# Attention scores from high and low halves of q and k in single-pass products, in a decoder layer whose instruction order is planned

## The chip, the cores and the metric

The kernel runs on one core of a Trainium2 chip. The metric is the device time of one execution in microseconds (us). The engines are TensorE (PE; PEld is its loading of the stationary operand), VectorE (DVE), ScalarE (ACT), GpSimd (POOL) and SyncE (SP), which here only issues the transfers.

## The reference

The layer has three parts, each followed by a residual sum and a layernorm, for 32 sequences of 256 tokens and 256 channels.

```python
x = layernorm(x + mamba(x))            # state-space block, 512 inner channels, 16 states, chunks of 64
x = layernorm(x + cross_attention(x, ctx_1024))
x = layernorm(x + experts(x))          # 8 experts by position, 256 -> 704 -> 256, silu(gate) * up

# the state-space block: u = silu(conv(x W_in)), delta = softplus(...), then for each chunk of 64
carry = exp(delta * A) * carry + delta * B * u         # over the tokens of the chunk
y = sum_n(carry * C);  y = y * silu(res);  out = y W_out

# the cross attention, 16 heads of 16 channels
scores = q k^T / sqrt(16);  attn = softmax(scores);  out = (attn v) W_o
```

All inputs and outputs are float32.

## The kernel before

**The order is planned.** The whole program is one pool of work that the author writes as generators ("chains"), one for each kind of work: `pres` and `steps` (projections and sizes of the state-space block), `decays`, `scan`, `weighted` and `sums` (the recurrence), `mixes` (output projection and first layernorm), `queries`, `keys_ahead`, `keys`, `maxima`, `attns`, `finishes` (attention), and for the experts `fetches`, `inputs`, `units` and `seconds`, twice. When the program is built, `in_order` keeps an account of the time on each engine. `spend` adds a duration to an engine, the yields tell when a chain can go on and on which engine it issues next, and the chain that can start first is stepped. The order of the instructions on every engine is what comes out, and it is fixed. The durations of the account are constants (`MM`, `EV`, `VE`, `CV`, `GP`, and numbers in the calls of `spend`). All transfers go through SyncE's one queue, in the order of the account (`dma`).

**The recurrence** has 512 steps, 16 for each sequence. A step loads delta and delta*u spread over 128 partitions (`ld`, two transfers of 256 KB), ScalarE takes the exponents (`da`, L573), VectorE multiplies (`bu`, L602) and scans 1024 elements (`h`, L621), GpSimd multiplies `h` by C (L637), and after four steps TensorE sums the states (`y`, L651) and VectorE gates the sum (`yg`, L667). Loads run three steps ahead, six `h` buffers exist.

**Attention.** Each sequence's q and k are made as 256 channels x 256 tokens (`q_flat`, `k_flat`, by `biased`), written to DRAM (`heads`, `k_all`) and read back by `spread_heads` into `qT` and `kT`. These have 64 rows for each head (`HR`), two heads side by side on the partitions (rows 0 and 64) and eight groups along the free axis. Of a head's 64 rows 16 hold its channels, the rest are zero in `qT`; `kT` has a one in row 63. `maxima` makes the scores of two heads in one call of `scores` (four products of 128x256, contraction over 63 rows), VectorE takes the maximum of each query (`tops`, L838), TensorE transposes the maxima, ScalarE negates them (`rows`, L847), and they go through DRAM into row 63 of `qT`. Then `attns` calls `scores` with k on the left, over 64 rows, so that the product holds score minus maximum, and ScalarE takes the exponent (`es`, L894). The products with v (`ps_oT`, L863) give output and sum together. A half of the heads (8) is one unit of this work. `scored` tells when a half of `qT` and `kT` can be overwritten.

**Experts.** 32 units of work (UNITS) of 256 columns; the last eight handle two experts on 128 columns each. A unit needs the finished second layernorm of its sequences, of the last four for the last four units. `ps_h` (L1133) and `ps_down` (L1212) are its products. They have the lowest rank when banks of PSUM are handed out (`take`; five banks).

The change touches `heads` (weights of q and k at the start), `rest`, `spread_heads`, `keys_ahead`, `queries`, `scores`, `maxima`, `attns`, a buffer of `finish` and the constants.

Of the kernel before, what the change touches and what calls it, by code (L numbers as in the profile page):

```python
# [7 lines left out]

F32 = mybir.dt.float32
AF = mybir.ActivationFunctionType  # L10
ALU = mybir.AluOpType
AX = mybir.AxisListType
# [3 lines left out]
P = 128  # L16
B, L, D = 32, 256, 256
# [5 lines left out]
NQ = NS // NL  # L23
GB = 2
# [8 lines left out]
NG = 4  # L33
# [64 lines left out]
def decoder_kernel(ctx: ExitStack, tc: tile.TileContext, a: dict, out: bass.AP):  # L98
# [4 lines left out]
    def dma(dst, src):  # L103

        nc.sync.dma_start(dst, src)
        spend("SP", ISSUE)
# [10 lines left out]

    k_all = dram.tile([B, D, L], F32, name="k_all")
    v_all = dram.tile([B, L, D], F32, name="v_all")

# [44 lines left out]

    def heads(n):

        w = wp.tile([P, 2, D], F32, tag="w_" + n, name="w_" + n)
        src = a["w_" + n].rearrange("(k p) (h c) -> p k h c", p=P, c=32)
        for k in range(2):  # L170
            dst = w[:, k].rearrange("p (h c) -> p h c", c=DK)
            dma(dst, src[:, k, :, :DK])
        bias = wp.tile([P, 2], F32, name="b_" + n)
        for g in range(NG):
            r = 64 * (g % 2)
            src = a["b_" + n].rearrange("(j c) g -> j c g", c=32)[:, :DK, g : g + 1]
            dma(bias[r : r + 64, g // 2 : g // 2 + 1], src)
        return w, bias
# [29 lines left out]

    later = []
    now, dma = dma, lambda dst, src: later.append((dst, src))  # L210
    w_k, b_k = heads("k")
    w_v = weight("w_v", D, D)
    b_out = row("b_out")
    w_out = weight("w_out", DI, D)
    w_q, b_q = heads("q")
    w_o = weight("w_o", D, D)
# [53 lines left out]

    kT = keep.tile([P, HG, L], F32, name="kT")
    last = small.tile([P, 1], F32, tag="ln_st", name="last")
    at = ident.rearrange("p (j c) -> p j c", c=HR)[:, :, HR - 1]
    nc.vector.tensor_reduce(last, at, AX.X, ALU.add)
    nc.vector.tensor_copy(kT.rearrange("p g t -> p (g t)"), last.to_broadcast([P, HG * L]))
    qT = keep.tile([P, HG, L], F32, name="qT")
    nc.gpsimd.memset(qT, 0.0)

# [27 lines left out]

    MM = 0.47
    EV = {1: 0.47, 2: 0.6, 4: 1.06}
    VE = {1: 0.41, 2: 0.69, 4: 1.23}
    CV = 0.565  # L310
    GP = {1: 0.7, 2: 1.27, 4: 2.36}

    def layernorm(tiles, t):

        n = len(tiles)
        mv = small.tile([P, n, 2], F32, tag="ln_mv", name="ln_mv")
        for i, x in enumerate(tiles):
            st = small.tile([P, 6], F32, tag="ln_st", name="ln_st")
            nc.vector.bn_stats(st, x)
            nc.vector.bn_aggr(mv[:, i, :], st)  # L320
        yield spend("DVE", 0.6 * n, t), "POOL"
        rstd = small.tile([P, n, 1], F32, tag="ln_rstd", name="ln_rstd")
        nc.gpsimd.tensor_scalar_add(rstd, mv[:, :, 1:2], EPS)  # L323
        nc.gpsimd.tensor_tensor(rstd, rstd, power[:, :n, :], ALU.pow)
        off = small.tile([P, n, 1], F32, tag="ln_off", name="ln_off")
        nc.gpsimd.tensor_tensor(off, mv[:, :, 0:1], rstd, ALU.mult)
        nc.gpsimd.tensor_scalar_mul(off, off, -1.0)
        yield spend("POOL", 1.5), "ACT"
        for i, x in enumerate(tiles):
            nc.scalar.activation(  # L330
                x, x, AF.Identity, bias=off[:, i, :], scale=rstd[:, i, :]
            )
        return spend("ACT", 0.6 * n)

# [29 lines left out]
    def rest():  # L364

        while later:
            yield 0.0, "SP"
            dma(*later.pop(0))

    xps, dds, sress, bcds, ygs, us, spread, silus = {}, {}, {}, {}, {}, {}, {}, []  # L370
# [175 lines left out]
    def decays():  # L546
# [15 lines left out]
        for i in range(STEPS):  # L562
# [8 lines left out]
            for g in range(GB):  # L571
                for q in range(NQ):
# [5 lines left out]
                    )  # L578
            decayed[i] = spend("ACT", GB * NQ * 0.5)

    read = {-1: 0.0}

    def scan():
# [4 lines left out]
        for i in range(STEPS):  # L588
# [39 lines left out]
            )  # L628
            recurred[i] = spend("DVE", 2.29)
            read[i] = max(multiplied, decayed[i])  # L630
# [45 lines left out]
    scored = {}  # L676

    def spread_heads(b, dst, d, t, there):

        yield t, "SP"  # L680
        for half in range(2):
            if b:
                yield lambda: max(t, scored[b - 1, half]) if (b - 1, half) in scored else None, "SP"
            for j in range(2):
                src = d.rearrange("(i g j c) t -> i j c g t", i=2, j=2, c=DK)[half, j]
                dma(dst[HR * j : HR * j + DK, 4 * half : 4 * half + 4, :], src)
            there[b, half] = clock.at["SP"] + LANDING
# [3 lines left out]
    def keys_ahead():  # L691

        for b in range(B):
# [14 lines left out]
            done(1, tk)  # L708
            yield tk, "SP"
            dma(k_all[b].rearrange("(m p) t -> p m t", p=P), flat)  # L710
            yield from take(1, rank, t0)
# [77 lines left out]
    def queries():  # L789
        for b in range(B):  # L790
# [12 lines left out]
            done(1, tq)  # L803
            yield tq, "SP"
            d = bcd.tile([D, L], F32, tag="heads", name="heads")
            dma(d.rearrange("(m p) t -> p m t", p=P), flat)
            yield from spread_heads(b, qT, d, clock.at["SP"] + LANDING, qts)

    def scores(heads, left, right, n):


        ss = [bank("s").rearrange("p (t n) -> p t n", t=2) for _ in heads]
        for t in range(2):
            for h, s in zip(heads, ss):
                g, r = h // 2, HR * (h % 2)
                nc.tensor.matmul(  # L816
                    s[:, t, :],
                    left[r : r + n, g, t * P : (t + 1) * P],
                    right[r : r + n, g, :],
                    start=True,  # L820
                    stop=True,
                )
        return ss, spend("PE", 2 * MM + 0.2)

    def maxima():

        for i in range(2 * B):
# [5 lines left out]
            while h < 8:  # L833
                yield from take(2, 2, t0)
                ss, ts = scores(range(8 * half + h, 8 * half + h + 2), qT, kT, HR - 1)
                for s in ss:
# [8 lines left out]
            yield spend("PE", 0.2), "ACT"  # L845
            rows = unit2.tile([H, P], F32, tag="rows", name="rows")
            nc.scalar.activation(rows, ps, AF.Identity, scale=-1.0)  # L847
            t = spend("ACT", 0.35)
            done(1, t)
            yield t, "SP"  # L850
            d = bcd.tile([2, 4 * L], F32, tag="tops", name="tops")
            dma(d.rearrange("j (i n) -> (j i) n", n=P), rows)
            yield clock.at["SP"] + LANDING, "SP"
            dst = qT[HR - 1 :: HR, 4 * half : 4 * half + 4]
            dma(dst.rearrange("j g t -> j (g t)"), d)
            tts[b, half] = clock.at["SP"] + LANDING
# [17 lines left out]
    def attns():  # L874

        for n in range(2 * B):
# [4 lines left out]
            for g in range(3):  # L881
                ess = []
                while g < 2 and len(ess) < 4:
                    yield from take(2, 2, tq)
                    h = 8 * half + 4 * g + len(ess)
                    ss, ts = scores(range(h, h + 2), kT, qT, HR)
                    if g and not ess:
# [36 lines left out]
    def finish(b):  # L924
# [27 lines left out]
        yield t, "ACT"  # L952
        aT = unit1.tile([P, 2, L], F32, tag="aT", name=f"aT_{b}")
        nc.scalar.copy(aT, ps)
# [387 lines left out]
```

## Time and profile before

| what | value |
|---|---|
| median of 3 runs | 2744.92 us (2738.03 to 2745.47) |
| the profiled execution | 2743.78 us |
| its span, first to last instruction | 2742.0 us |
| TensorE busy | 2466.3 us, 90% |
| VectorE busy | 2380.6 us, 87% |
| ScalarE busy | 2043.4 us, 75% |
| GpSimd busy | 1643.7 us, 60% |
| moved by DMA | 505.86 MB, 64.8% of the 16 engines' time |
| mean granted clock of TensorE | 0.959 |

"Busy" for TensorE counts a product from its start to the modelled end, so overlapping products count once, and a wide busy time is not the same as full use. A line of the group and timeline views gives line, engine, operation, output<-inputs, shapes and count; a line of the waits gives who waited for whom, the microseconds in total, how often, and the longest. A float32 product is two records in the trace, each with its own load.

### The profile page before, as it was taken

To read this page: it belongs to the slowest core of one execution; us is meant where nothing else is said; L and a number is where in the kernel's file an instruction comes from. 1 tells how busy PE (TensorE), PEld (TensorE's weight loads), DVE (VectorE), ACT (ScalarE), POOL (GpSimd) and SP (SyncE) were. 2 spreads that over 40 slices of the span, in tenths; PEclk is the share of its full clock that TensorE was granted. 3 is DMA by queue.
4 is the path that set the end of the run, shared out by engine and by line. 5 is a ranking of instruction groups with operands and counts; after the bars stand their busy time and mean duration, and the time that the engine had idled before them with its cause. 6 is when DMAs were issued, how large, how long until landed. Compare 5 with 4: busy or idle time off the path is not lost.

```text
span 2742.0 us, 48659 instructions
## 1 busy us (share of the span) xinstructions
PE 2466.3 (90%) x16964; PEld 1705.3 (62%) x16964; DVE 2380.6 (87%) x2413; ACT 2043.4 (75%) x4327; POOL 1643.7 (60%) x1145
## 2 busy tenths in 40 slices
PE   5788989889899899989998989999999899998988
PEld 4565666566566666666666666665666566666767
DVE  4999999999999999999999999999999899896212
ACT  6887888888778878887878778888788788674331
POOL 4775766666666666575666665666666666553000
PEclk8899999999999999998999999999999999999999
DMA  7866666666676666676666666667666566666464
GB/s 203 228 199 176 193 187 181 189 191 191 187 199 186 181 167 190 176 197 177 167 198 187 198 175 186 187 177 195 190 197 179 163 172 180 185 174 181 150 195 144
DMA packets 491497, 505.86 MB, mean 184 GB/s; under 512 B 177204, under 2 KB 339252, under 8 KB 491252
## 3 DMA queue, kind: packets, MB, share of 16 engines
q1 hardware_dynamic: 491252, 502.75, 64.8%
q8 instruction: 135, 2.21, 0.4%
q14 instruction: 110, 0.90, 0.1%
HBM read 426.07 MB, written 76.55 MB: 183 GB/s over the span
## 4 chain that ended last, share of the span: by engine, by line
PE 29%; DVE 11%; ACT 8%; DMA 5%; issue 3%; POOL 1%; SPq 1%; DVEq 0%; ACTq 0%; POOLq 0%
PE ps_h L1133 8%; PE s L816 6%; DVE h L621 5%; PE ps_down L1212 4%; ACT da L573 3%; PE y L651 3%; DVE bu L602 2%; DVE tops L838 2%; PE ps_in L349 2%; PE ps_oT L863 2%; DMA ld<-dd 1%; DMA xe<-x2d 1%; PE ps_out L349 1%; PE ps_qk L349 1%; ACT es L894 1%
## 5 line engine op out<-in xcount | busy, mean ns | idle before, releaser
L637 POOL TENSOR_TENSOR h<-h,c_bc 128x1024 f32<-128x1024 f32 x512 | 1209.1, 2362 | 740.6 <-DVE h L621 627.0
L621 DVE TENSOR_TENSOR_SCAN h<-da,bu 128x1024 f32<-128x1024 f32 x512 | 1168.9, 2283 | 50.4 <-ACT da L573 5.8
L573 ACT ACTIVATE da<-ld,a_neg 128x252 f32<-128x252 f32 x2048 | 864.6, 504 | 188.3 <-DVE h L621 138.4
L602 DVE TENSOR_TENSOR bu<-ld,b_bc 128x1024 f32<-128x1024 f32 x512 | 626.1, 1223 | 19.9 <-DMA ld<-dd 8.0
L816 PE MATMUL s<-kT,qT 63*128 63x256 f32 x2048 | 345.4, 416 | 45.6 <-DVE tops L838 22.8
L894 ACT ACTIVATE es<-s 128x512 f32<-128x512 f32 x512 | 277.9, 594 | 140.6 <-PE s L816 75.9
L838 DVE TENSOR_REDUCE tops<-s 128x2 f32<-128x512 f32 x512 | 325.2, 677 | 41.6 <-PE s L816 41.1
L1133 PE MATMUL ps_h<-x2T,w 128*128 128x256 f32 (+2 forms) x1536 | 343.5, 368 | 9.5 <-ACT es L894 1.7
L816 PE MATMUL s<-qT,kT 64*128 64x256 f32 x2048 | 313.8, 405 | 22.5 <-DMA qT<-tops 13.0
L651 PE MATMUL y<-h,sel_y 128*32 128x256 f32 x4096 | 280.8, 397 | 52.3 <-POOL h L637 36.9
L816 PEld LDWEIGHTS s<-kT,qT 63*128 63x128 f32 x2048 | 213.8, 193 | 151.9 <-DVE tops L838 50.8
L1133 PEld LDWEIGHTS ps_h<-x2T,w 128*128 128x128 f32 (+1 forms) x1536 | 246.7, 186 | 89.7 <-issue 35.1
L349 PE MATMUL ps_in<-xT,w_in 128*128 128x256 f32 x1024 | 258.4, 397 | 8.7 <-ACT da L573 2.6
L816 PEld LDWEIGHTS s<-qT,kT 64*128 64x128 f32 x2048 | 200.9, 189 | 102.3 <-issue 39.6
L651 PEld LDWEIGHTS y<-h,sel_y 128*32 128x32 f32 x4096 | 131.8, 113 | 177.4 <-POOL h L637 55.1
L349 PEld LDWEIGHTS ps_in<-xT,w_in 128*128 128x128 f32 x1024 | 192.8, 196 | 60.4 <-issue 12.9
L420 POOL TENSOR_TENSOR u<-u,shifted 128x512 f32<-128x512 f32 x128 | 151.4, 1183 | 39.7 <-ACT u L407 34.7
L323 POOL TENSOR_SCALAR ln_rstd<-ln_mv 128x2 f32<-128x2 f32 x96 | 20.9, 218 | 254.2 <-DVE ln_mv L320 250.0
L407 ACT ACTIVATE shifted<-ps_in,tap_b,conv_w 128x256 f32<-128x256 f32 x256 | 130.8, 567 | 22.5 <-PE ps_in L349 10.9
L863 PE MATMUL ps_oT<-es,v 128*32 128x256 f32 x2048 | 142.4, 391 | 3.7 <-DVE h L1197 1.2
L349 PE MATMUL ps_out<-w_out,yg 128*128 128x256 f32 x512 | 117.6, 383 | 0.4 <-DVE yg L667 0.4
L375 ACT ACT_TABLE_LOAD x90 | 115.5, 1283 | 1.4
(135 smaller groups left out, 2987.5 us busy)
## 6 DMA issues: line engine op xcount, KB each, us to landing
ld<-dd SPq DMA_DIRECT2D x1024, 256.0 KB
w<-in_w SPq DMA_DIRECT2D x128, 352.0 KB
x<-in_x SPq DMA_DIRECT2D x64, 256.0 KB
dd<-delta SPq DMA_DIRECT2D x32, 512.0 KB
dd<-u SPq DMA_DIRECT2D x32, 512.0 KB
w<-in_w SPq DMA_DIRECT2D x32, 384.0 KB
w13y<-in_w SPq DMA_DIRECT2D x32, 352.0 KB
c_bc<-bcd SPq DMA_DIRECT2D x64, 128.0 KB
```

The costliest lines, as they stand in the source:

```text
L349: nc.tensor.matmul(ps[:, j, :], l, r, start=(k == 0), stop=(k == len(terms) - 1))
L420: nc.gpsimd.tensor_tensor(u[:, cc], u[:, cc], at, ALU.add)
L573: nc.scalar.activation(da[:, g, q].rearrange("p (k t) -> p k t", t=CHUNK)[:, :, 1:], loads[i][:, 0, g].rearrange("p (k t) -> p k t", t=CHU ...
L602: nc.vector.tensor_tensor(bu, loads[i][:, 1].unsqueeze(2).to_broadcast([P, GB, NQ, L]), b_bc.unsqueeze(1).to_broadcast([P, GB, NQ, L]), AL ...
L621: nc.vector.tensor_tensor_scan(h.rearrange("p g q t -> p (g q t)"), das_of.pop(i).rearrange("p g q t -> p (g q t)"), bu.rearrange("p g q t ...
L637: nc.gpsimd.tensor_tensor(hs[i], hs[i], c_bc, ALU.mult)
L651: nc.tensor.matmul(y[32 * j : 32 * j + 32, :], sel_y[:, g, :], hs[i - NJ + 1 + j][:, g, q, :], start=(g == 0 and q == 0), stop=(g == GB - ...
L816: nc.tensor.matmul(s[:, t, :], left[r : r + n, g, t * P : (t + 1) * P], right[r : r + n, g, :], start=True, stop=True,)
L838: nc.vector.tensor_reduce(top[:, h % 2, h // 2, :], s, AX.X, ALU.max)
L863: nc.tensor.matmul(oT[32 * j : 32 * j + 32, :], v[:, k, 4 * g + j, :], ess[j][:, k, :], start=(k == 0), stop=(k == 1), tile_position=(0, 3 ...
L894: nc.scalar.activation(es, s, AF.Exp, scale=1.0 / DK**0.5)
L1133: nc.tensor.matmul(ps[:m, i, :], w_tiles[u, which, e][k][:, f * P : f * P + m], right, start=(k == 0), stop=(k == 1),)
```

## The change

Queries and keys are split into a high part, rounded to the type float32r, and a low part, the rest. A head's 64 rows now hold its 16 channels four times, in `kT` as high, low, high, low and in `qT` as high, high, low, low, so that one product over 64 rows sums all four combinations of the parts. The products run in float32r. The maximum no longer sits in a row of `qT`; it is split likewise and kept in `mT`, and is added to the scores by a second product with a selecting matrix `pick`, accumulated in PSUM. The weights of q and k are read as before into a raw buffer and brought into a new order of channels by GpSimd at the start. The splits run on GpSimd (`parts_of`). Constants of the account are changed to durations from a trace.

The diff, cut to its core:

```diff
-    k_all = dram.tile([B, D, L], F32, name="k_all")
+    k_all = dram.tile([B, 2, 2, P, L], F32, name="k_all")
...
+        def ordered():
+            for k in range(2):
+                for i in range(2):
+                    at = slice(i * P, (i + 1) * P)
+                    nc.gpsimd.tensor_copy(
+                        w[:, k, at].rearrange("p (j c g) -> p g j c", j=2, c=DK),
+                        raw[:, k, at].rearrange("p (g j c) -> p g j c", j=2, c=DK),
+                    )
+            spend("POOL", 1.6)
...
-    kT = keep.tile([P, HG, L], F32, name="kT")
...
-    qT = keep.tile([P, HG, L], F32, name="qT")
-    nc.gpsimd.memset(qT, 0.0)
+    kT = keep.tile([P, HG, L], F32R, name="kT")
+    qT = keep.tile([P, HG, L], F32R, name="qT")
+    mT = keep.tile([P, L], F32R, name="mT")
+    nc.gpsimd.memset(mT.bitcast(F32), 0.0)
+    pick = keep.tile([P, HG], F32R, name="pick")
...
-    MM = 0.47
-    EV = {1: 0.47, 2: 0.6, 4: 1.06}
-    VE = {1: 0.41, 2: 0.69, 4: 1.23}
-    CV = 0.565
-    GP = {1: 0.7, 2: 1.27, 4: 2.36}
+    MM = 0.49
+    EV = {1: 0.42, 2: 0.56, 4: 1.05}
+    VE = {1: 0.41, 2: 0.66, 4: 1.225}
+    CV = 0.535
+    GP = {1: 0.7, 2: 1.23, 4: 2.36}
...
-            decayed[i] = spend("ACT", GB * NQ * 0.5)
+            decayed[i] = spend("ACT", GB * NQ * 0.43)
...
+    def parts_of(n, b, full, t, d):
+
+        hi = unit1.tile([P, 2, L], F32R, tag="hi", name=f"{n}_hi_{b}")
+        lo = unit1.tile([P, 2, L], F32R, tag="lo", name=f"{n}_lo_{b}")
+        yield t, "POOL"
+        nc.gpsimd.tensor_copy(hi, full)
+        nc.gpsimd.tensor_tensor(lo, full, hi.bitcast(F32), ALU.subtract)
+        t = spend("POOL", 2 * GP[2])
+        yield t, "SP"
+        for s, part in enumerate((hi, lo)):
+            dma(d[:, s].rearrange("i p t -> p i t"), part.bitcast(F32))
...
-                src = d.rearrange("(i g j c) t -> i j c g t", i=2, j=2, c=DK)[half, j]
-                dma(dst[HR * j : HR * j + DK, 4 * half : 4 * half + 4, :], src)
+                src = d[half, :, HR * j : HR * (j + 1), :].rearrange("s (c g) t -> s c (g t)", g=NG)
+                for s in range(2):
+                    r = HR * j + 2 * DK * s
+                    at = dst[r : r + 2 * DK, NG * half : NG * (half + 1), :]
+                    at = at.bitcast(F32).rearrange("p g t -> p (g t)")
+                    if dst is qT:
+                        dma(at, src[s].unsqueeze(0).to_broadcast([2, DK, NG * L]))
+                    else:
+                        dma(at, src)
...
-            yield tk, "SP"
-            dma(k_all[b].rearrange("(m p) t -> p m t", p=P), flat)
+            yield from parts_of("k", b, flat, tk, k_all[b])
...
-    def scores(heads, left, right, n):
+    def scores(heads, left, right, lowered):
...
                 nc.tensor.matmul(
                     s[:, t, :],
-                    left[r : r + n, g, t * P : (t + 1) * P],
-                    right[r : r + n, g, :],
+                    left[r : r + HR, g, t * P : (t + 1) * P],
+                    right[r : r + HR, g, :],
                     start=True,
-                    stop=True,
+                    stop=not lowered,
                 )
-        return ss, spend("PE", 2 * MM + 0.2)
+            for h, s in zip(heads, ss):
+                g, r = h // 2, HR * (h % 2)
+                if lowered:
+                    nc.tensor.matmul(
+                        s[:, t, :],
+                        pick[r : r + HR, g : g + 1].to_broadcast([HR, P]),
+                        mT[r : r + HR, :],
+                        start=False,
+                        stop=True,
+                    )
+        return ss, spend("PE", 0.7 if lowered else 0.4)
...
-            rows = unit2.tile([H, P], F32, tag="rows", name="rows")
+            rows = unit1.tile([H, P], F32, tag="rows", name="rows")
...
-            yield t, "SP"
-            d = bcd.tile([2, 4 * L], F32, tag="tops", name="tops")
-            dma(d.rearrange("j (i n) -> (j i) n", n=P), rows)
+            yield t, "POOL"
+            both = unit1.tile([H, 2, P], F32R, tag="both", name="both")
+            nc.gpsimd.tensor_copy(both[:, 0], rows)
+            nc.gpsimd.tensor_tensor(both[:, 1], rows, both[:, 0].bitcast(F32), ALU.subtract)
+            yield spend("POOL", 0.8), "SP"
+            d = bcd.tile([2, H, P], F32, tag="tops", name="tops")
+            dma(d.rearrange("s x n -> x s n"), both.bitcast(F32))
             yield clock.at["SP"] + LANDING, "SP"
-            dst = qT[HR - 1 :: HR, 4 * half : 4 * half + 4]
-            dma(dst.rearrange("j g t -> j (g t)"), d)
+            for j in range(2):
+                r = HR * j + 8 * half
+                src = d[:, 8 * j : 8 * j + 8, :].rearrange("s (g t) n -> s g (t n)", t=2)
+                dma(mT[r : r + 8].bitcast(F32), src)
...
-        aT = unit1.tile([P, 2, L], F32, tag="aT", name=f"aT_{b}")
+        aT = unit1.tile([P, 2, L], F32, tag="x1T", name=f"aT_{b}")
```

The order of instructions that comes out has on TensorE 3072 score products instead of 2048, on GpSimd 264 instructions more, on SyncE 392 transfers more, and the work of the chains stands in other places on every engine.

## The prediction

> **What bounds the kernel now.** I read the busy times first.
>
> ```profile
> PE 2466.3 (90%) x16964; PEld 1705.3 (62%) x16964; DVE 2380.6 (87%) x2413; ACT 2043.4 (75%) x4327; POOL 1643.7 (60%) x1145
> ```
>
> Two engines look full, so the span has to be cut into stages: the start, up to the end of the last scan, and the rest.
>
> ```profile
> core 0: us, PE busy (x) PEld busy (x) DVE busy (x) ACT busy (x) POOL busy (x), PEclk, DMA share, GB/s
> 0.00:62.00 62.00, 36.96 (x138) 26.93 (x142) 24.87 (x23) 35.00 (x68) 28.73 (x39) 0.82 0.77 198
> 62.00:2513.40 2451.40, 2231.39 (x15433) 1518.18 (x15425) 2302.89 (x2272) 1937.37 (x4127) 1595.20 (x1056) 0.96 0.66 185
> 2513.40:2742.00 228.60, 198.00 (x1399) 160.22 (x1397) 52.85 (x119) 71.03 (x133) 19.76 (x50) 0.93 0.54 172
> ```
>
> The long middle belongs to VectorE (94% busy) with TensorE close behind (91%). The last 229 us belong to TensorE alone. So a faster TensorE is worth, in the middle, only what VectorE waits for it, and in the tail what is on the chain. VectorE's waits up to the last scan:
>
> ```profile
> DVE tops L838 <- PE s L816: 22.5, 26, 3.5
> DVE yg L667 <- PE y L651: 16.1, 14, 3.0
> DVE xe L1224 <- PE ps_down L1212: 13.0, 4, 6.9
> DVE a_neg L560 <- ACT a_neg L558: 11.0, 1, 11.0
> DVE x L964 <- PE ps_o L349: 10.2, 9, 2.6
> ```
>
> With the smaller ones in the same view (ps_h 4.3 + 2.5 + 1.4 + 1.1, ps_oB 3.6, b_bc 3.5) VectorE waits 78 us for TensorE. The y products wait themselves for GpSimd (36.9 us in TensorE's waits), so about 62 us are TensorE's own lateness. The other VectorE idle time there, some 62 us, is about 0.1 us ahead of each scan and small steps; no change of TensorE touches it. That caps the middle's gain near 2.5%.
>
> The price of one score call (two heads, four products, eight records, since a float32 product is two records) comes from the timeline of TensorE:
>
> ```profile
> 2466.20 0.66 PE L935 MATMUL ps_oB<-ident,oS 128*128 128x128 f32 x4
> 2466.70 0.60 PE L1118 MATMUL ps_xe<-ident,xe 128*128 128x128 f32 x4
> ...
> 2485.35 1.13 PE L816 MATMUL s<-kT,qT 63*128 63x256 f32 x8
> 2486.41 1.99 PE L1133 MATMUL ps_h<-x2T,w 128*128 128x256 f32 x8
> ```
>
> From start to next start a call takes 1.06 us. It already runs two heads side by side on rows 0 and 64: eight records in the time of four at 226 ns (a plain 128x256 product shows 16 records in 3.62 us). So the change can't gain by side-by-side work, only by fewer passes.
>
> **The change, part by part.** All is added to the profiled execution, 2743.8 us (span 2742.0); the median of the three runs is 2744.9, so the two agree.
>
> *Score calls.* There are 256 calls for the maxima and 256 for the exponents. Today both cost 1.06. After, a maxima call is four single products, an exponent call eight (four more lower the scores by the maximum). No row shows such a product. Lower bound: one pass is a quarter of 2 x 226 = 113 ns; two heads side by side, plus the 0.15 by which the last record (376) outlasts the pace (226): 2 x 0.113 + 0.15 = 0.38 and 0.60. Upper bound: the transposes above, single records with a 128-column load each, pace 0.50 for four, so 0.50 and 1.00. I take 0.45 and 0.80, between, because the transposes do not use two row groups. Saved: 256 x 0.61 + 256 x 0.26 = 223 us (bounds 159 to 292), all on TensorE, about 215 in the middle. [...]
>
> *Work that moves.* In the changed order 88 fewer ps_h products, 18 fewer ps_down and two fewer ps_oT calls stand behind the last y: 88 x 0.25 + 18 x 0.48 + 2 x 1.0 = 33 us of feed-forward work goes from the tail into the middle. TensorE in the middle is then 2231 - 215 + 33 = 2049, or 85% of about 2410. With it VectorE gets 9 us more ahead of the last scan (counted from its order, row by row: ps_h products at 0.68 and 0.41, layernorm steps at 0.41 and 0.18): +9. Of the 62 us of TensorE's lateness I let 40 go, two thirds, as the queue is left 15% free instead of 9%; bounds 0 and 62. What is late next is y behind GpSimd. -40.
>
> *The split.* GpSimd gets 64 pairs (copy, subtract) on 128x512. The subtract is 1.18 to 1.27 by the rows of u and x; a one-input copy lies between a memset's pace (0.95 for 1024, so 0.48) and 1.27. I take 2.4 a pair, by the nearer tensor_tensor: 154 us, and 64 small pairs on 16x128 at about 0.6 (between the 0.2 of the 128x2 steps and 0.7): 38 us. GpSimd goes from 1595 to about 1785 of the middle, 74%. Its idle time hides that: it waits 627 us for the scan. A pair put between two multiplications of h (2.36 in a step of about 4.7) delays the next by 2.4 less the 1.3 idle in front of it, 1.1 us. It reaches VectorE only where a y waits for that very multiplication, one step in four: 16 x 1.1 to 2.4, that is 18 to 38 us on y, of which today 16.1 of 36.9 arrive at yg: 8 to 17.
>
> *Transfers.* k and q each write 512 instead of 256 KB and read 1 MB instead of 256 KB in a batch: 2 MB more, 64 in all, 13% on 505.86 MB; SyncE issues 392 more, at the 0.42 us of a qT issue 165 us, beside the 669 us for which its queue waits on bu. The loads of ld stand behind them in that queue; VectorE waits 8.0 us for ld today, covered by three steps of lead (14 us). If that cover went, each of 64 bursts would cost its 1 MB at 283 GB/s (184 at a share of 0.65), 3.6 us. Split and transfers together: +10 (0 to 60). Transfers also wait now for GpSimd instead of ScalarE: behind the waiting issue stand ld loads, two or three a step.
>
> *Start.* In ScalarE's order the second batch's sres and Silu (1.6 + 4.7 us) now stand ahead of the first decay, where 3.5 us of waiting for ld lay; part is given back at 70 us, where the same steps held up the scan by 2.6. Eight more bias issues at 0.55 fit into SyncE's pause before 33 us. +2 (-2 to +5). The memsets of kT and qT fall in idle time.
>
> *Tail.* From the last y (2517.8) to the store of the last x (2635.9) are 118 us, 108.7 of them TensorE busy, and the 106 after it don't change (the same four units). TensorE's work there becomes 108.7 - 33 - 14 x 0.26 - 8 x 0.61 = 67. But the chain of the last batch is about as long: ps_out 5.5, add and statistics 2, GpSimd 1.5, normalise 1.1, transposes and copy 1.2, ps_qk 4.6 behind ps_down, bias 0.8, split 2.4, two transfers 8.7, four maxima calls among feed-forward work 10, transpose and rows 1.2, transfers 7, then three exponent calls, maxima of the second half, its 1.2 and 7, four calls 5, and 11 to the store: 73. Interleaved badly, 88: -30 (bounds -45 and 0).
>
> Sum: 2743.8 - 40 + 9 + 10 + 2 - 30 = 2695.
>
> *The clock.* Where TensorE was busy 60% (the first 62 us) the granted clock was 0.82; at 91% it was 0.96. If 85% brought 0.90, 2049 us would grow by 137 and fill the queue again: no gain in the middle. The gaps now are one to three us, so I expect it to stay at 0.95 or above. [...]
>
> **The rivals.** *More than that:* calls at the lower bound and all 62 us of lateness gone, tail at its floor: 2743.8 - 62 + 9 + 2 - 45 = 2648. For it speaks that most feed-forward units end two to eight y calls (of four steps) earlier in the new order. *Tail only:* lateness is the order's, not the queue's; the 40 stays: 2735. Against it speaks that waits for s and ps_down are the largest. *GpSimd gets in the way:* the split delays y and, through SyncE's one queue, the ld loads. Price: 64 pairs of 2.4 are 154; from 59 us on (the 10 that I take and the forecast's gain of 49) it decides. With half of it on the scan, 77, instead of 10: 2762. For it: VectorE waits for y are already half GpSimd's. Against: 627 us of GpSimd's waiting. *Not one pass:* if such a product costs as much as today's, 256 calls double, +271 on TensorE, 2502 in a middle of 2451; TensorE then bounds: about 2743.8 + 51 + the 62 of waits, 2860 at most.
>
> **How the numbers follow.** The forecast has 0.50 (own range 2665 to 2718), more than that 0.15 (2625 to 2665), tail only 0.15 (2718 to 2750), GpSimd 0.15 (2745 to 2800), not one pass 0.05. 0.3%, 8 us, is about what a measurement of this kernel can tell from no change. Faster by more is the first two and half of the third: 0.73; the same 0.09; slower 0.18. The range 2635 to 2760 leaves out a part of the first rival, most of the fourth and the last, 0.2 in all.
>
> **What would show it.** Right: a maxima call pacing 0.38 to 0.50 and an exponent call 0.60 to 1.00, TensorE's busy share in the middle below 88%, VectorE's waits for s, ps_down and ps_o at most half, the last scan ending near 2485, and from the last y to the last store 80 to 95 us. Wrong: VectorE waiting for y or ld by over 60 us (GpSimd), score calls at 1 us or more, or a granted clock near 0.90.

## The result, and the profile after

The changed kernel takes 3758.03 us (median of 4 runs, 3756.77 to 3759.43) against 2745.01 before: a ratio of 1.3699, 95% interval 1.3675 to 1.3722. The forecast was 2695. The profiled span is 3755.9 us, the mean granted clock 0.799 (before 0.959).

The page first, busy times of the engines and the line of the transfers' queue (packets, MB, share of 16 DMA engines):

```profile
PE 2539.1 (68%) x15940; PEld 1741.0 (46%) x15940; DVE 2399.6 (64%) x2413; ACT 2044.4 (54%) x4329; POOL 1802.9 (48%) x1409
...
q1 hardware_dynamic: 507860, 570.90, 52.6%
```

No engine is full any more. Nor are the DMA engines: 14% more bytes move, but the share fell from 64.8% to 52.6%. Something makes everybody wait, and it isn't bandwidth. The stages (columns as in the same view of before; the last scan now ends at 3528.9):

```profile
62.00:3528.90 3466.90, 2332.18 (x14711) 1576.85 (x14712) 2335.53 (x2292) 1950.82 (x4157) 1752.59 (x1313) 0.79 0.53 153
3528.90:3755.90 227.00, 165.12 (x1084) 132.03 (x1083) 44.21 (x101) 51.32 (x99) 20.40 (x48) 0.85 0.48 147
```

All of the loss lies in the middle, 3467 us instead of 2451. VectorE's waits there:

```profile
DVE tops L892 <- PE s L860: 503.2, 106, 21.1
DVE yg L695 <- PE y L679: 143.1, 47, 11.5
DVE x L1024 <- PE ps_o L373: 119.2, 17, 17.3
DVE bu L630 <- DMA ld<-dd: 70.8, 20, 15.5
```

VectorE names TensorE as before, 941 us in all instead of 78. But TensorE was said to be the engine that gets faster, so the reader has to ask what TensorE and the others wait for. From the waits of all engines and of SyncE's queue:

```profile
ACT da L601 <- DMA ld<-dd: 880.5, 131, 31.7
...
PE s L860 <- DMA qT<-heads: 296.9, 56, 14.6
```

```profile
SPq L106 <- DVE bu L630: 236.9, 115, 10.1
SPq L106 <- DMA kT<-k_all: 194.2, 106, 4.2
SPq L106 <- DMA qT<-heads: 174.0, 96, 3.9
```

The same two readings before:

```profile
ACT da L573 <- DMA ld<-dd: 44.4, 17, 6.0
SPq L105 <- DVE bu L602: 668.7, 311, 8.1
```

There the queue had time to spare. Now it waits for the loads of kT and qT themselves, its spare time is down to 237 us, and `ld` comes late. The chain of waits between 1080 and 1118 us shows how long a transfer takes (start, duration, what); this `ld` was issued right behind four loads of kT:

```profile
1080.58 12.29 DMA ld<-dd
...
1104.70 12.68 DMA qT<-heads
```

Nearly all packets of 4096 bytes in the trace are these loads (16384 of 16640, 182 ns each in the mean). A burst of 128 of them, the four loads of a half of q or of k, 512 KB, takes 12.2 us (median); where two such bursts meet, the 1 MB takes 22.6 us. The packets' times summed and divided by the time of the bursts give 2.01, so about two are under way at any time (exactly two for 90% of it). This is read here as two of the 16 DMA engines at work on these loads, and "on two engines" below stands for it; which engine a packet ran on, the trace does not record.

The access patterns of these loads begin with the two parts of k, or with a repeat of two for q. That this leading two is the cause was a guess at this point; the first run below tests it.

### The profile page after: what moved, and what is told of

It reads as the page before. It is cut to its first block, busy times and chain, and to the rows that moved or that the text cites. A ratio compares the mean times of both kernels' runs of the same rounds, so it can differ in the third digit from the quotient of the medians.

```text
span 3755.9 us, 47492 instructions
## 1 busy us (share of the span) xinstructions
PE 2539.1 (68%) x15940; PEld 1741.0 (46%) x15940; DVE 2399.6 (64%) x2413; ACT 2044.4 (54%) x4329; POOL 1802.9 (48%) x1409
## 3 DMA queue, kind: packets, MB, share of 16 engines
q1 hardware_dynamic: 507860, 570.90, 52.6%
## 4 chain that ended last, share of the span: by engine, by line
DMA 42%; PE 24%; ACT 10%; SPq 9%; DVE 7%; issue 4%; POOL 4%; ACTq 0%; DVEq 0%; POOLq 0%
DMA ld<-dd 13%; DMA qT<-heads 10%; SPq L106 9%; DMA mT<-tops 5%; PE ps_h L1193 5%; ACT da L601 4%; PE y L679 3%; PE ps_in L373 3%; PE s L860 3%; PE ps_down L1272 2%; DVE h L649 2%; POOL h L665 2%; DMA x2d<-x 2%; DVE tops L892 2%; DMA w<-in_w 2%
## 5 line engine op out<-in xcount | busy, mean ns | idle before, releaser
L601 ACT ACTIVATE da<-ld,a_neg 128x252 f32<-128x252 f32 x2048 | 863.0, 502 | 981.1 <-DMA ld<-dd 880.5
L892 DVE TENSOR_REDUCE tops<-s 128x2 f32<-128x512 f32 x512 | 325.1, 681 | 521.3 <-PE s L860 520.9
L860 PE MATMUL s<-kT,qT 64*128 64x256 f32 x1024 | 201.6, 404 | 420.5 <-DMA qT<-heads 296.9
L1193 PE MATMUL ps_h<-x2T,w 128*128 128x256 f32 (+3 forms) x1632 | 402.9, 397 | 35.4 <-DMA w<-in_w 17.1
L679 PE MATMUL y<-h,sel_y 128*32 128x256 f32 x4096 | 324.5, 434 | 111.1 <-POOL h L665 89.7
L860 PEld LDWEIGHTS s<-kT,qT 64*128 64x128 f32 x1024 | 126.9, 236 | 520.0 <-issue 390.8
L1193 PEld LDWEIGHTS ps_h<-x2T,w 128*128 128x128 f32 (+1 forms) x1632 | 287.0, 207 | 121.7 <-issue 43.6
L373 PE MATMUL ps_in<-xT,w_in 128*128 128x256 f32 x1024 | 296.8, 442 | 15.2 <-ACT xT L413 5.5
L870 PE MATMUL s<-mT,pick 64*128 64x256 f32 x1024 | 182.3, 328 | 162.7 <-DMA mT<-tops 162.4
L860 PE MATMUL s<-qT,kT 64*128 64x256 f32 x1024 | 205.9, 359 | 33.8 <-ACT es L954 16.7
L870 PEld LDWEIGHTS s<-mT,pick 64*128 64x128 f32 x1024 | 137.0, 222 | 172.4 <-DMA mT<-tops 172.1
L860 PEld LDWEIGHTS s<-qT,kT 64*128 64x128 f32 x1024 | 132.9, 215 | 113.2 <-issue 41.2
```

What stands on the lines that cost most here:

```text
L373: nc.tensor.matmul(ps[:, j, :], l, r, start=(k == 0), stop=(k == len(terms) - 1))
L601: nc.scalar.activation(da[:, g, q].rearrange("p (k t) -> p k t", t=CHUNK)[:, :, 1:], loads[i][:, 0, g].rearrange("p (k t) -> p k t", t=CHU ...
L679: nc.tensor.matmul(y[32 * j : 32 * j + 32, :], sel_y[:, g, :], hs[i - NJ + 1 + j][:, g, q, :], start=(g == 0 and q == 0), stop=(g == GB - ...
L860: nc.tensor.matmul(s[:, t, :], left[r : r + HR, g, t * P : (t + 1) * P], right[r : r + HR, g, :], start=True, stop=not lowered,)
L870: nc.tensor.matmul(s[:, t, :], pick[r : r + HR, g : g + 1].to_broadcast([HR, P]), mT[r : r + HR, :], start=False, stop=True,)
L892: nc.vector.tensor_reduce(top[:, h % 2, h // 2, :], s, AX.X, ALU.max)
```

## The experiments

Medians are compared by their ratio to the kernel before, which ran beside each. "The 16-engine kernel" below is the first one, and "on 16 engines" stands for patterns that begin with 16 (mT: with 4), whatever the number of engines at work.

**All loads on more engines.** The same bytes, pieces and instruction order, with the channels ahead of the repeat (the rows of mT, and with them the columns of `pick`, change places too):

```diff
-  src = d[half, :, HR*j : HR*(j+1), :].rearrange("s (c g) t -> s c (g t)", g=NG)
+  src = d[half, :, HR*j : HR*(j+1), :].rearrange("s (c g) t -> c s (g t)", g=NG)
-  dma(at, src[s].unsqueeze(0).to_broadcast([2, DK, NG * L]))
+  dma(at, src[:, s].unsqueeze(1).to_broadcast([DK, 2, NG * L]))
-  src = d[:, 8*j : 8*j + 8, :].rearrange("s (g t) n -> s g (t n)", t=2)   # mT
+  src = d[:, 8*j : 8*j + 8, :].rearrange("s (g t) n -> g s (t n)", t=2)
...
```

> The changed kernel with the loads of kT, qT and mT written so that the outermost dimension of the source has 16 entries (kT, qT: the channels) or 4 (mT) instead of 2; the same bytes in the same 4 KB pieces, the same number of transfers, the same order of instructions. Theory A (the loads run on two of the 16 DMA engines because their outermost dimension is 2; 12 to 13 us for the four loads of a half): the four loads take 3 to 5 us, ScalarE's waits for ld fall from 880 to below 100 us, the granted clock returns from 0.80 to 0.94 or more, and the time is 2695, the sum of the forecast's other terms (2640 to 2750). Theory B (the 64 MB more): nothing changes, 3700 or more. Theory C (the float32r products or their gaps lower the clock by themselves): ld waits fall but the clock stays near 0.80 and the time stays above 3100. Theory D (GpSimd's split and the 392 more issues on SyncE's queue): above 3300, with VectorE waiting for y by hundreds of us.

Measured: 2861.86 us, ratio 1.0434 (1.0408 to 1.0459). A burst of 128 packets takes 3.2 us, one of 256 5.5 us, and 9.9 packets are under way at a time instead of two. Theory A explains 896 of the 1013 us lost; B, C and D, which all asked for more than 3100, fall. The time is not the 2695 of the forecast's other terms, though, and the clock is 0.89 and not 0.94: 117 us against the kernel before stay open. ScalarE's wait for `ld` and the stages of this run:

```profile
ACT da L601 <- DMA ld<-dd: 95.2, 48, 7.7
...
62.00:2662.00 2600.00, 2161.12 (x14692) 1480.28 (x14696) 2326.44 (x2292) 1954.98 (x4156) 1757.45 (x1313) 0.89 0.73 204
2662.00:2865.70 203.70, 164.10 (x1106) 131.37 (x1098) 44.43 (x101) 51.66 (x100) 20.48 (x48) 0.89 0.52 162
```

The tail is 25 us shorter than before, the middle 149 longer, 122 of which are VectorE waiting for TensorE (200 us instead of 78).

**Without the edit to mT; q alone; the planner told.** Three variations of the same question. In the first, the loads of mT stay on two engines. In the second, only qT is mended (`for n in range(2): dma(at[DK*n : DK*(n+1)], src[s])`). In the third nothing is mended, but the account charges 13 and 8 us instead of `LANDING`, 3.5 (one run each for the second and third).

> As the kernel with all loads on more engines, but the loads of mT (64 of 512 pieces of the same kind in a batch, two engines) left as in the changed kernel. Theory A: the mT loads carry an eighth of what kT and qT carry, so most is regained: 2700 to 2800, with TensorE's waits for mT below half of the 162 us. Theories B, C and D: as for the other kernel, above 3100.

> Only the loads of qT changed: two loads of 16 rows in place of each broadcast of two, so that q comes over 16 engines, with 128 more issues on SyncE's queue; kT and mT stay on two engines. Theory A: half of the slow bursts are gone (about 8300 pieces of 4 KB on two engines instead of 16640), and about half of the loss of 1014 us is back or somewhat more, as a lone slow burst of 6 us hides better: 3000 to 3250. Theory D (issues on SyncE's queue are what costs): not faster than the changed kernel, 3750 or more. Theory B: 3700 or more.

> The changed kernel with the planner's account told how long these loads take (13 us for kT and qT, 8 us for mT, instead of 3.5): the order of the instructions changes, the transfers are as slow as before. Theory A, with the loss through ld and the queue that all transfers share: the score calls move later and their waits (s for qT 297, for mT 162) fall, but ld stays late, so less than a third of the loss is back: 3400 to 3750. Rival (the order was only planned with a wrong landing time): nearly all is back, below 2900.

Measured: 2867.05 (ratio 1.0466, 1.0441 to 1.0491, not to be told from the 16-engine kernel, and like it above the range expected), 3378.71 and 3745.17 us. So kT and qT carry the loss, mT next to nothing. With half of the loads mended 379 of 896 us are back: less than expected, the remaining half costs more than half. Planning for late loads gives 13 us, 0.3%, by one run.

**Unread loads in the kernel before.** Is it the products that wait for these loads, or everything else? After each of its own loads of kT and qT the kernel before gets two more of 128 KB into a tile that nobody reads, 64 MB in all; the second run has `unsqueeze(1).to_broadcast([DK, 2, ...])` instead.

```diff
+  rows = a["x"][b].rearrange("(c q) d -> c (q d)", q=4)[:DK]
+  for s in range(2):
+      r = HR * j + 2 * DK * s
+      dma(spare[r : r + 2*DK], rows.unsqueeze(0).to_broadcast([2, DK, NG * L]))
```

> The kernel before with 16 more loads in each batch, 128 KB each in pieces of 4 KB (64 MB in all), behind its own loads of kT and qT, from x into a spare tile that nobody reads; the source begins with a repeat of two, as the loads of qT do in the changed kernel. What it is to tell: whether slow loads on two engines cost even where no product waits for them. Theory A1 (the two engines carry a share of ld and of everything else, and SyncE's queue stalls behind them): 3100 to 3600, ScalarE's waits for ld above 400 us, granted clock below 0.87. Theory A2 (it was the score calls waiting for their own operands): below 2820.

> The same 64 MB in the same pieces into the same spare tile, with the repeat of two moved behind the 16 channels. The forecast took 10 us for split and transfers together, 230 had the cover gone: by the forecast 2745 to 2765. By what leaving out half of these loads gave (46 us for 32 MB, from 2862 to 2816): 2790 to 2840.

Measured: 3777.41 us (ratio 1.3788, 1.3755 to 1.3821; more than the 3600 that was the most expected) and 2917.80 us (1.0644, 1.0610 to 1.0678). The waits of all engines in the first, then in the second, there with SyncE's queue:

```profile
ACT da L574 <- DMA ld<-dd: 877.8, 107, 27.3
DVE tops L843 <- PE s L821: 522.2, 118, 24.0
```

```profile
ACT da L574 <- DMA ld<-dd: 162.1, 59, 11.6
DVE tops L843 <- PE s L821: 130.1, 70, 10.7
...
SPq L105 <- DVE bu L603: 430.7, 219, 7.4
```

Without a single product that needs them, the loads on two engines cost 1037 us and give the changed kernel's picture in these two lines (880.5 and 520.9 there, over the whole run). Theory A1 holds: the loss comes through what shares the queue and the two engines. How much of it is the queue standing still and how much the two engines being shared, no run separates. (Each half overwrites the spare tile, so SyncE's queue also waits for these loads among themselves there; the 713 us of that wait are no measure of the changed kernel's, and that 1037 comes so near 1013 may be chance.) On 16 engines the same 64 MB still cost 177 us, more than either estimate. VectorE waits under 2 us for a transfer in the middle of that run and 15 for ScalarE, but 238 for TensorE instead of 78, while ScalarE waits 162 us for `ld` in the whole run instead of 44. So the loads seem to reach VectorE by way of ScalarE and TensorE; the links between were not followed one by one. The spare time of SyncE's queue, its wait for `bu`, fell from 669 to 431 us.

**What else could hold the 117 us: GpSimd, bytes, landing times.** Four kernels from the 16-engine one, the first three in its order. (1) The maximum in its high part alone, written by ScalarE as float32r, without `both`. (2) `lo` a tile of zeros, no subtraction. (3) As (2), and the loads with `s = 1` left out. (4) As (1), with the account told so and 5.5 us for landing.

> The kernel with all loads on more engines (2862 us), in the same order, with the maximum kept in its high part alone: ScalarE writes the negated maxima as float32r, GpSimd's 64 small pairs go (47 us, and 90 us in which GpSimd stands waiting for ScalarE's rows with the multiplications of h behind it), and each load of mT brings 4 rows of 1 KB instead of 8. Subtracting a rounded maximum changes no softmax, since output and sum hold the same factor. Still open are the 120 us between 2862 and the kernel before; VectorE waits 200 us for TensorE in the middle there against 78 before. Theory G (GpSimd's new waits make h, y and the attention late): 2790 to 2830, the wait of y for h falls from 50 to about 30 us. Theory K (TensorE's clock) or T (the 64 MB more of transfers): 2845 to 2870.

> The kernel with all loads on more engines, in the same order, without GpSimd's 64 subtractions of 128x512 (1.27 us each, 82 us): the low parts of q and k are zeros that are stored and loaded as before. Theory G: GpSimd is free earlier for h, VectorE's waits for TensorE fall by a third or more, 2790 to 2830. Theories K and T: 2845 to 2870.

> As the kernel without the subtractions, and the second load of each pair for kT and qT left out, so that half of the rows stay zero (low parts of q are left out of the scores): 32 MB less written into SBUF, 256 issues less. Theory T (the transfers): against the kernel without the subtractions another 40 to 80 us are back, 2740 to 2800; TensorE's waits for qT and ScalarE's for ld (31 and 95 us) fall by half. Theories K and G: within 20 us of the kernel without the subtractions.

> The kernel with the maximum in its high part alone, and the planner told so: no GpSimd work between the maxima and their transfers, and 5.5 us instead of 3.5 for the landing of kT, qT and mT (the loads of a half take 4.2 us after their issue). The order changes. If part of the loss is that TensorE's order puts score calls before their operands are there (45 us of waits for qT and mT): 20 to 50 us below the kernel with the maximum in its high part. If those waits only move: within 15 us of it.

Measured: 2857.04 (ratio 1.0416, 1.0382 to 1.0450), 2862.28 (1.0440), 2816.01 (1.0272, 1.0245 to 1.0300), 2859.83 (1.0433). GpSimd's 47 and 82 us, and the 90 us it stands waiting for `rows`, are worth nothing that can be measured: theory G falls. Half of the loads are worth 46 us, the 40 to 80 of theory T, though the time itself stays above its 2740 to 2800. A better landing time is worth nothing.

**The account's constants.** The changed kernel's constants put back in the 16-engine kernel, and its new constants put into the kernel before (`MM` 0.47 or 0.49 and the others of the diff).

> The kernel with all loads on more engines, with the constants of the planner's account as they were before the change. The order of the instructions differs, their number and kind do not. If the new constants were part of the loss: 2800 or less. If the loss lies in the score calls and the clock: within 30 us of 2862.

> The kernel before with the changed constants of the account alone. If the constants by themselves matter: more than 15 us from 2740, slower if they belong to the loss. If not: 2730 to 2755, the clock as before, 0.96.

Measured: 2882.49 (1.0514, 1.0485 to 1.0544) and 2744.01 (1.0002, 0.9985 to 1.0019). The new constants do nothing before, and are 0.8% better than the old ones in the changed kernel. They are no part of the loss.

**TensorE's clock.** The trace records when the granted clock was half: 226 us before, 1513 in the changed kernel, 634 in the 16-engine kernel. Work that nobody needs was added there, 115 us behind TensorE's waits for free banks, or ahead of `y`:

```diff
-  for t in range(2):
+  for t in range(2) if lowered else (0, 1, 0, 1):     # first kernel, in scores
...
+  for k in range(2):                                  # second kernel, in sums
+      nc.tensor.matmul(y, ident, w_q[:, k, :], start=True, stop=True)
```

> The kernel with all loads on more engines (2862 us), in the same order, but the four products of each of the 256 maxima calls are issued twice, the second time over the first: TensorE gets 256 times 0.45 us, 115 us, of work that nobody needs, just behind the waits for the VectorE that frees its banks. What it is to tell: whether the 120 us still missing against the kernel before come from TensorE's clock, which is at half speed for 634 us in the run of 2862 and for 226 us before, in stretches that follow 3.4 us pieces in which TensorE was less than half busy. Theory of the clock: with more work the pieces stay over half busy, the time at half clock falls to 350 to 500 us, the mean granted clock rises from 0.89 to 0.92 or more, and the time stays where it is or falls in spite of the 115 us: 2830 to 2870. Theory of the queue (TensorE's order and the waits of VectorE are what costs, the clock is only an onlooker): TensorE 85% busy in the middle takes up to half of the added work into the end: 2890 to 2930.

> The kernel with all loads on more engines, in the same order, with two plain float32 products of 128x256 (0.9 us together, 128 times, 115 us in all) ahead of each call of y, into y's own bank and overwritten by y: the work that nobody needs stands inside TensorE's wait for GpSimd's h. Theory of the clock: y is behind 14 of the 101 falls to half clock, so these vanish and the half clock falls by some 80 us, the time by 0 to 30: 2830 to 2870, unless the products delay y where h was ready. Theory of the queue: y is 0.9 us later wherever h was ready, VectorE's wait for y grows from 44 to 80 us or more, 2890 to 2930.

Measured: 2871.48 (1.0491, 1.0463 to 1.0518), clock 0.906, 542 us at half clock; and 2892.48 (1.0569, 1.0528 to 1.0610), clock 0.905, 552 us. By the ratios 16 of 115 us reach the end in the first, 37 in the second. In the first the half clock shrinks by 92 us, less than the theory of the clock asked (350 to 500 us left, and a clock of 0.92), and the time lies just outside its range. In the second it shrinks by 82, as that theory asked, but the time is the one of the theory of the queue. Filler does not decide it: it brings the clock up a little and stands in the way a little.

**The single passes by themselves.** The kernel before, same order, same transfers, with kT and qT declared float32r, unsplit:

```diff
-  kT = keep.tile([P, HG, L], F32, name="kT")
+  kT = keep.tile([P, HG, L], mybir.dt.float32r, name="kT")       # qT likewise
...
```

> The kernel before, in its order, with kT and qT given to TensorE as float32r without a split, so that each score product is a single pass (the low parts are left out of the scores); no transfer, no GpSimd work, no order changes. TensorE saves some 512 times 0.6 us, 300 us. By the forecast (two thirds of the 62 us that VectorE waits for TensorE go, the clock stays at 0.95 or above, less in the tail): 2670 to 2715. Theory K (pieces of 3.4 us in which TensorE is under half busy halve its clock, so what is saved is given back): half clock for 450 us or more instead of 226, granted clock below 0.93, VectorE's waits for TensorE no shorter than 78 us: 2725 to 2770.

> The kernel before with both: single passes without a split, and the 64 MB of unread loads over 16 engines (the low parts are left out of the scores). If the two costs only add, its distance from the kernel before is the sum of the two others, within 20 us. If a lower clock and later loads feed each other: 30 us or more above the sum, near the 2862 of the changed kernel with all loads on more engines.

Measured: 2753.30 us (ratio 1.0050, 1.0031 to 1.0069), clock 0.901, 544 us at half clock; and 2907.52 (1.0603, 1.0567 to 1.0638). These are theory K's numbers, and the two costs about add (13 and 177 make 190, measured 167). The middle of the first run, then five pieces of 3.41 us of TensorE in it (stretch, its length, busy, granted clock, DMA share, GB/s):

```profile
62.00:2533.00 2471.00, 2067.50 (x13503) 1384.47 (x13495) 2305.06 (x2273) 1937.78 (x4129) 1596.12 (x1056) 0.90 0.65 184
```

```profile
core 0: us, PE busy (x), PEclk, DMA share, GB/s
1093.06:1096.47 3.41, 2.61 (x18) 1.00 0.73 232
1096.47:1099.89 3.42, 2.76 (x30) 1.00 1.02 273
1099.89:1103.30 3.41, 1.35 (x14) 1.00 0.53 132
1103.30:1106.71 3.41, 3.40 (x26) 0.50 0.58 196
1106.71:1110.13 3.42, 3.42 (x17) 1.00 0.77 226
```

TensorE was busy for 1.35 us of the third piece, the longest pause in it 1.27 us, and got half the clock for the fourth, where it had work for all of it. Counted over this run: 56 of 86 falls to half clock follow a piece in which TensorE was less than half busy, and only 6 of the 558 pieces at full clock with no fall behind them were that idle. In the kernel before it is 32 of 38, and 8 of 696. The other 30 falls of this run follow pieces that were 50 to 77% busy, so half is no sharp bound. VectorE waits 93 us for TensorE instead of 78, although TensorE's busy time in the middle is 164 us shorter. By the prices some 300 us of products were saved; over the whole span TensorE's busy time fell by 179 us and its time at half clock rose by 318. (In the fourth piece above 26 products of y took 3.58 us; 32 of them took 1.93 at full clock in the kernel before.)

**Planned for the cheaper calls.** Was that the order's fault? The maxima alone in single passes, exponents in float32; and both in single passes; each with `spend("PE", 0.45)` for such a call.

> The kernel before with the maxima alone in single passes of float32r on the unsplit q and k (a maximum may be a little off, since output and sum share it), the exponents in float32 as before, no added transfer, and the planner's account told 0.45 us for a maxima call, so that the order is made for it. 256 times 0.6, 154 us, of TensorE go. By the forecast's sum (the lateness of TensorE on VectorE, and feed-forward work that moves out of the tail): 2700 to 2730. Theory K, as the single passes alone in the old order showed it (2753, half clock for 544 us): within 10 us of 2741, with half clock for 350 us or more.

> The kernel with unsplit single passes for maxima and exponents (2753 in the old order; the low parts are left out of the scores), with the account told 0.45 us for every score call: the order is planned anew, with 300 us less of TensorE in the account. If the 13 us lost there were the old order's: 2690 to 2720. If the clock takes back what is saved in any order: 2735 to 2765, half clock for 500 us or more.

Measured: 2741.50 (1.0004, 0.9989 to 1.0020), 402 us at half clock; and 2733.40 (0.9969, 0.9952 to 0.9987), 541 us. The first is what theory K gave. The second lies between its two ranges, nearer to the clock's: the order made for the cheaper calls is worth 0.8% against the old one (1.0050), but not the 2690 to 2720. The stages of the second:

```profile
62.00:2543.00 2481.00, 2104.55 (x13804) 1417.84 (x13797) 2318.16 (x2294) 1966.09 (x4173) 1598.87 (x1064) 0.90 0.65 187
2543.00:2734.00 191.00, 150.35 (x992) 121.74 (x990) 42.81 (x97) 48.12 (x93) 17.04 (x42) 0.89 0.49 153
```

The tail is 38 us shorter than before, the middle 30 longer. It is the only version below the kernel before, by 0.3%, and it leaves out the low parts.

## Why the prediction was wrong

By the ratios the runs take the change apart like this (each times 2742 us, near the medians before): single passes, with an order made for them, -8; all the rest of the change on 16 engines (the transfers, the split, the products that lower the scores, and the order that came of them), from 0.9969 to 1.0434, +127; the same loads on two engines, from 1.0434 to 1.3699, +895.

*Transfers: the step that failed.* The prediction wrote "Split and transfers together: +10 (0 to 60)" and priced a burst by its bytes, "1 MB at 283 GB/s ..., 3.6 us". Two things were wrong. The bytes were taken to spread over all DMA engines; they went two packets at a time, 22.6 us for 1 MB (5.5 in the 16-engine kernel, at 9.9 packets). That, 895 us, was outside every rival: "GpSimd gets in the way" named SyncE's one queue, but GpSimd's work was worth nothing that the runs on 16 engines could measure. The sign set for that rival, VectorE waiting over 60 us for y or `ld`, did appear (143 and 71 us): it tells that they are late, not who makes them late. And even on 16 engines the cover was not there. It was read from VectorE's 8.0 us of waiting for `ld`, but `ld` is read first by ScalarE, which already waited 44 us for it. In the kernel before with the loads spread out ScalarE's wait for it grew to 162 us, and VectorE's wait for TensorE from 78 to 238. The prediction's price for lost cover, 64 times 3.6, 230 us, was of the right size: 177 in the kernel before, and at most about the 127 in the changed one, of which half of the loads is shown to be 46 and the rest is not taken apart.

*The clock: the second step that failed.* "The gaps now are one to three us, so I expect it to stay at 0.95 or above." It was 0.90 with nothing changed but the passes, the very number that the prediction feared, at TensorE 84% busy in the middle. That gaps of this length leave the clock alone was the author's estimate, and no run shows it: 16 gaps of more than 3.4 us stand against 86 falls in this run (7 against 38 in the kernel before), and the half-empty piece shown ahead of a fall has no pause above 1.27 us. The prediction had priced this case itself ("no gain in the middle") and set it aside.

*Lateness, -40.* With the order of before, TensorE saves 164 us of busy time in the middle and VectorE waits 15 us longer for it; planned anew it waits 94 us. That the less busy TensorE ran more of its time at half clock is shown (226 us of the run with 2231 us busy in the middle, 544 with 2067); that this alone is what eats the gain is not, since neither filler (0.906 at most) nor anything else tried with single passes (0.93 at most) brought the clock back to 0.96. The alternative, that VectorE's waits come from the order and the chains between engines and not from TensorE's load, would leave the same result, and the run with the maxima doubled (115 us more work, 16 us later) speaks for it as well.

*The prices of the calls* were right or pessimistic. From the timeline of TensorE in the 16-engine kernel:

```profile
1491.90 0.38 PE L860 MATMUL s<-qT,kT 64*128 64x256 f32 x2
1492.12 0.28 PE L870 MATMUL s<-mT,pick 64*128 64x256 f32 x2
1492.24 0.28 PE L860 MATMUL s<-qT,kT 64*128 64x256 f32 x2
1492.36 0.28 PE L870 MATMUL s<-mT,pick 64*128 64x256 f32 x2
1492.57 0.66 PE L1178 MATMUL ps_xe<-ident,xe 128*128 128x128 f32 x4
...
1516.15 0.51 PE L860 MATMUL s<-kT,qT 64*128 64x256 f32 x4
1516.59 1.99 PE L1193 MATMUL ps_h<-x2T,w 128*128 128x256 f32 x8
```

Within a call the pairs of single-pass products from the second on follow each other after 0.12 us (0.22 from the first to the second), so the quarter of a float32 product in the lower bound (113 ns), which was an estimate, is about right. An exponent call takes 0.67 us from its start to the next product's (0.80 predicted), a maxima call 0.44 (0.45). *Tail:* -30 predicted, -25 in the 16-engine kernel. *Moved work on VectorE:* +9 predicted, +23 in that kernel (2326 us busy in the middle against 2303). *GpSimd:* a pair of 1.88 us (0.61 and 1.27) instead of 2.4, and without effect. Taken together: the rival "tail only", priced at 2735, comes near the products without the transfers (2733), in part by luck: there the tail gave 38 us instead of 30 and the middle took 30, and that the waits are the order's, its reason, is not shown. The memory side decided.

## What to carry to other kernels

Before a transfer is priced by its bytes, look at the outermost dimension of its access pattern and at how many of its packets are under way at a time (here 2.01 with a leading two, 9.9 with 16); a layout trick such as a leading repeat of two costs nothing in bytes and made these loads about four times as long (12.2 us for 512 KB against 3.2). Read the cover of a shared queue from the first reader of what stands behind it, not from the engine that bounds the kernel (here ScalarE's 44 us, not VectorE's 8). And when a change takes work off a TensorE that is 90% busy, price it once with a lower clock as well: here, with the passes alone changed, the mean granted clock went from 0.96 to 0.90, and 164 us less busy time were worth nothing in the middle, whether by the clock alone or not.

## What was not expected of the hardware

Loads that nobody reads, begun with a repeat of two, cost 1037 us for 64 MB, against 177 us for the same 64 MB with 16 in front, and ScalarE's wait for `ld`, on the same queue, grew from 44 to 878 us, against 162. TensorE's clock fell to half in stretches of 3.41 us and multiples of it, mostly after pieces of that length in which it was less than half busy (56 of 86 falls with single passes, 32 of 38 before); in the piece shown, no pause was longer than 1.27 us.
